# A mixture-of-experts stage that adds straight into the output, with a bound on the row index

## The chip, the core and the metric

The kernel runs on one core of a Trainium2 chip. The engines are named as the profile names them: PE (TensorE, matrix products and transposes), DVE (VectorE), ACT (ScalarE), POOL (GpSimd) and SP (SyncE, which here only starts transfers). Each engine works through its own list of instructions in order and waits at semaphores for the others. Transfers go through sixteen DMA engines; those with a list of row indices are started by POOL, whose software writes their descriptors, and nearly all others by SP. The metric is the time of one execution on the device, in microseconds (us).

## The reference

The input is x with 4 batches of 512 tokens and 256 features, all in 32-bit floats. Three residual steps follow each other:

```
x = x + 0.5 * ffn(layernorm(x))
x = x + attention(layernorm(x))          # 16 heads, low-rank queries and keys, rotary part
x = x + 0.5 * ffn(layernorm(x))

def ffn(x):                              # 8 experts, each token goes to 2 of them
    w, idx = top_k(x @ gate, 2);  w = softmax(w)
    h = silu(x @ w0[e]) * (x @ w1[e])    # 256 -> 512, for each chosen expert e
    return sum over the chosen e of  w[e] * (h @ wo[e])     # 512 -> 256
```

Both ffn steps use the same weights. Every token takes part in two experts, so each ffn step adds 4096 weighted rows into 2048 rows.

## The kernel before, in words

**Tiles.** For each of the two ffn stages (f = 0 before the attention, f = 1 after it) the (token, expert) pairs are sorted by expert into tiles of 128 slots. There are always 36 tiles. Four of them are shared: their lower 64 slots belong to one expert and their upper 64 to another. The rest have one expert each. `list_tiles` makes, for each tile, a column of row indices (`idx`; for shared tiles two columns in `half_idx`, one for each half) and a column of weights. A slot that holds no token gets an index from 2048 up, a "spare" row behind the tokens; the slots of the other half in `half_idx` point to spare rows too. Therefore the normed tokens `xn_d` and the sums `acc_d` in DRAM have more than 2048 rows (`NTOK` is 2048, `P` is 128), and `clear` writes zeros to the spare rows at the start, on POOL's queue.

**One tile.** `ffn_tiles` runs over the tiles. For each one, `gather` (POOL, indirect DMA, L1057) fetches 128 rows of `xn_d`; `turn` transposes them on PE; `hidden` makes the two hidden products and `it`; `turn_hidden` transposes `it`; `project` multiplies with wo, scales by the weights on DVE (`yo`, L1176) and hands the tile to `scatter` (POOL, indirect DMA with addition, L1153). For a shared tile there are two scatters, one with each column of `half_idx`; the second is put off to the next round (`later`). A tile's gather is issued two rounds ahead, and further ahead from tile `final` on. PE's order is fixed by hand: the hidden product of tile j, the transposes of tile j+1, then the projection of tile j-1.

**Order of the scatters.** Two scatters may add to the same rows, so each waits until the one before it has landed. The scatters form a chain on POOL, in which every step lasts from the start of one to the start of the next.

**Stage one** adds to `acc_d[0]`, into which x was copied. **The attention** loads x per batch from there, adds its own result in SBUF, and `finish_x` (SP) writes each batch to `acc_d[1]`.

**Stage two** has 17 tiles that are full and need the first three batches only, then 8 tiles in turn shared and full (tiles 17 to 24), then 11 more (tiles 25 to 35, `final` is 25). The first 25 tiles add to `acc_d[1]`. When tile 24 has been projected, SP copies `acc_d[1]` into the output in four pieces (L1192); the output is the kernel's result in DRAM, `flat_out` in the code. Tiles 25 to 35 then add to the output itself. They come after the copy in the chain; `HELD = 2` puts the scatters of tiles 25 and 26 off until that of tile 27, so that the gathers of the next tiles get ahead of them in POOL's list. For tiles from 25 on `list_tiles` makes indices that stay below 2048, also in tiles that no expert uses (their weights are zero).

The lines that decide where a scatter goes:

```
direct = final is not None and j >= final
dst = flat_out if direct else acc_d[f][: res["rows"] + two_rows, :]
...
if not direct or j >= final + HELD:
    scatter(held)
```

Of the kernel before, what the change touches and what calls it, by code (L numbers as in the profile page):

```python
# [9 lines left out]
F32 = mybir.dt.float32  # L10
# [6 lines left out]
P = 128  # L17
# [25 lines left out]
def kernel(  # L43
# [18 lines left out]
    nc = tc.nc  # L62
    B, S, D = x.shape
# [8 lines left out]
    NTOK = B * S  # L72
# [27 lines left out]
    qp = ctx.enter_context(tc.tile_pool(name="q", bufs=4))  # L100
    pp = ctx.enter_context(tc.tile_pool(name="p", bufs=2 * NT + 1))
    ptp = ctx.enter_context(tc.tile_pool(name="pt", bufs=2 * NT))
    ap = ctx.enter_context(tc.tile_pool(name="o", bufs=2))
    dp = ctx.enter_context(tc.tile_pool(name="dram", bufs=1, space=bass.MemoryType.DRAM))
# [3 lines left out]


    xn_d = [dp.tile([NTOK + P, D], F32, name=f"xn_d{f}") for f in range(2)]  # L110
    acc_d = [dp.tile([NTOK + 2 * P, D], F32, name=f"acc_d{f}") for f in range(2)]


    tab_d = [dp.tile([P * P, 2], F32, name=f"tab_d{f}") for f in range(2)]
# [2 lines left out]
    def rows(t, b):  # L117
        return t[b * S : (b + 1) * S, :].rearrange("(t p) d -> p t d", p=P)

    xs = {}  # L120

    def load_x(b, src):
        xs[b] = xpool.tile([P, NT, D], F32, tag="x", name="x")
        nc.sync.dma_start(xs[b], src)
# [53 lines left out]
    half_idx = counted("half_idx", [P, 2, NSHARED], [[P, 2], [0, NSHARED]], NTOK, 1, I32)  # L178
# [35 lines left out]
    nc.gpsimd.memset(zero, 0.0)  # L214

    def clear():
        for t in (xn_d[0], acc_d[0], xn_d[1], acc_d[1]):
            for r in range(NTOK, t.shape[0], P):
                nc.gpsimd.dma_start(t[r : r + P, :], zero)
        for t in tab_d:  # L220
            nc.gpsimd.dma_start(t.rearrange("(c s) v -> c (s v)", s=P), zero)
# [281 lines left out]
    class Phase:  # L503
# [17 lines left out]
        def scatter(self, s, k, t):  # L521

            nc.gpsimd.memset(self.between, 0.0)
            put = nc.gpsimd.indirect_dma_start(
                out=tab_d[self.f],
                out_offset=bass.IndirectOffsetOnAxis(ap=s["s_i"][:, k, t : t + 1], axis=0),
                in_=s["pair"][:, k, t, :],
                in_offset=None,
            )

            for other in self.written:
                tc.declare_no_dep(put.ins, other.ins, reason="other slots")
            self.written.append(put)
# [502 lines left out]

        return res, parts()

    HELD = 2
    flat_out = out.rearrange("b s d -> (b s) d")  # L1040

    def ffn_tiles(f, jobs, final=None):

# [96 lines left out]
        def turn_hidden(it):  # L1143
# [4 lines left out]
            nc.scalar.copy(iT, pt)  # L1148
            return iT

        def scatter(these):
            for dst, idx, y in these:
                nc.gpsimd.indirect_dma_start(  # L1153
                    out=dst,
                    out_offset=bass.IndirectOffsetOnAxis(ap=idx, axis=0),
                    in_=y,
                    in_offset=None,
                    compute_op=ALU.add,
                )
            these.clear()  # L1160

        def project(j, off, iT):
            res, i = jobs[j]
            py = ps_p.tile([P, D], F32, tag="p", name="py")
            two = shared(j)
            for m in range(MC):
                first_half(two, py, iT[:, m, :], w_sb[2][:, bass.ds(off + m * D, D)], m, MC)
                if two:
                    wo = copies[j][2 * DC + m // 2][:, m % 2 * D : (m % 2 + 1) * D]
                    second_half(py, iT[:, m, :], wo, m, MC)  # L1170
            copies.pop(j, None)
            direct = final is not None and j >= final

            pool, tag = (qp, "q") if direct else (ptp, "pt")
            y = pool.tile([P, D], F32, tag=tag, name="yo")
            nc.vector.tensor_scalar_mul(y, py, res["w"][:, i : i + 1])  # L1176
            two_rows = P if two else 0
            dst = flat_out if direct else acc_d[f][: res["rows"] + two_rows, :]
            idx = res["idx"][:, i : i + 1]
            if two:  # L1180

                held.append((dst, half_idx[:, 0, i : i + 1], y))
                later.append((dst, half_idx[:, 1, i : i + 1], y))
            else:
                held.append((dst, idx, y))
            if not direct or j >= final + HELD:
                scatter(held)
            if final is not None and j == final - 1:

                for r in range(0, NTOK, NTOK // 4):  # L1190
                    r = slice(r, r + NTOK // 4)
                    nc.sync.dma_start(  # L1192
                        flat_out[r, :].rearrange("(p r) d -> p (r d)", p=P),
                        acc_d[f][r, :].rearrange("(p r) d -> p (r d)", p=P),
                    )

        held, later = [], []
        gather(0)
        gather(1)
        yield -1  # L1200
# [3 lines left out]
        for j in range(n):  # L1204
            gather(j + 2)
            if final is not None and j >= final:

                gather(j + 3)
                if j > final:
                    gather(j + 4)  # L1210
            scatter(later)
            if j == n - 1:

                off, it = hidden(j, lambda: project(*todo))
                todo = None
            else:
                off, it = hidden(j)
            yield j
            turn(j + 1)
            yield j  # L1220
            if todo is not None:
                project(*todo)
            yield j
            todo = (j, off, turn_hidden(it))
            yield j
# [240 lines left out]
    def finish_x(i):  # L1466
        b, h = items[i]
        if h == NH - 1:
            nc.sync.dma_start(rows(acc_d[1], b), xs[b])

    def rest_of(res, n):

# [24 lines left out]
    for half in range(2):  # L1497
# [2 lines left out]

    nc.sync.dma_start(mark_d, list_a["w"][:, :n_a])
    nc.sync.dma_start(
        acc_d[0][:NTOK, :].rearrange("(p r) d -> p (r d)", p=P),
        x.rearrange("b s d -> (b s) d").rearrange("(p r) d -> p (r d)", p=P),
    )
    load_attention()
# [9 lines left out]
    for j in tiles:  # L1516
        place = place + 1 if place < 4 else 1
        beside.at(place)
        if j < n_a - 2:
            beside.step(3)  # L1520
            if j == n_a - 3 and place == 4:
                beside.finish()
        elif j == done + 1 and place == 1:
            load_x(0, rows(acc_d[0], 0))
        elif j == done + 2 and place == 1:
            beside.add(prepare(0), put_queries(0), put_queries(1))
        elif j > done + 2:
            beside.step(2 if place % 2 == 0 else 1)
        if j == len(jobs) - 1:
            if place == 1:  # L1530
                beside.finish()
            put_scores(place - 1)
            put_divide(place - 1)
    load_x(1, rows(acc_d[0], 1))
    for k in range(NT, NT + LEAD):
        put_scores(k)
        put_divide(k)
# [19 lines left out]
    for i, (b, h) in enumerate(items):  # L1557
        if h == 2:
            if b > 0:
                load = None  # L1560
                if b + 1 < B:
                    load = lambda b=b: load_x(b + 1, rows(acc_d[0], b + 1))
                routed = {}
                beside.add(route_one(two, b - 1, routed, load))
            if b + 1 < B:
                beside.add(prepare(b + 1))
            if b > 0:
                beside.add(scatter_one(two, routed))
            if b == B - 1:
                beside.add(listing)  # L1570
        for kc in range(NT):

            at = NT * (h % 2) + kc
            beside.at(at, at in (6, 7, 0, 1), LITTLE if late and ROOM[at] < 1.0 else ROOM[at])
            k = (i + 1) * NT + LEAD + kc
            if at != 1 or i == 0:
                put_scores(k)
            if at == 0 and i > 0:

                put_scores(k + 1)  # L1580
                put_weigh(i - 1, range(NT))
                put_divide(k)
                beside.step(PARTS[at])
            if at == 5:

                put_divide(k - 1)
            pts[i, kc] = turn_probs(probs[i], kc)
            for f in late:
                f()
            late.clear()  # L1590
            if at == 1:
                asked.add(put_queries(i // 2 + 2))
                beside.step(PARTS[at])
            elif at == 4 and h % 4 == 1 and i > 1:
                late.append(put_out(i - 2, 0))
            elif at == 6 and h % 4 == 1 and i > 1:
                late.append(put_out(i - 2, 1))
                late.append(lambda i=i: finish_x(i - 2))
            asked.step(ASKED[at])
            if at == 0 and i == 0:  # L1600
                put_divide(k)
            if at > 1 or at == 0 and i == 0:
                beside.step(PARTS[at])
        probs.pop(i)
# [87 lines left out]
```

## Time and profile before

| | |
|---|---|
| time, three runs | 1111.03 us median (1108.27 to 1111.64) |
| the profiled execution | 1107.51 us, with a span of 1105.7 us |
| mean clock granted to PE | 0.99 |
| busy: PE, DVE, ACT, POOL | 1053.1, 562.1, 476.5, 586.7 us |
| POOL: indirect gathers of 128 rows (L1057) | 72, mean 1006 ns |
| POOL: indirect scatters with addition (L1153) | 53 + 16 to `acc_d`, 11 to the output; 1582, 1575 and 1569 ns |
| scatter, issue to landing (median) | 3.7 to 3.8 us |
| copy of sums to the output (SP) | 4 transfers of 512 KB, 5.6 us to landing |

A row of POOL's DMA_INDIRECT tells how long POOL took for the instruction; the data lands later. The time to landing is counted from the issue. In a timeline, a number in square brackets is how long the engine sat idle before the instruction, followed by what ended that idle time; "issue" means that nothing shown in the profile ended it.

### The profile page before, as it was taken

The numbers are of one execution on the slowest core, as the hardware profiler recorded it, in microseconds if no ns is written. First come the engines' busy times: TensorE is split into PE (matmuls) and PEld (weight loads), VectorE is DVE, ScalarE is ACT, GpSimd is POOL, SyncE is SP. The second block draws the span as 40 slices with busy tenths as digits, with TensorE's granted clock in tenths as the row PEclk, the third lists the DMA queues.
The fourth block names the chain that finished last, engine by engine and source line by source line (L and its number), as shares of the span: only waits on it lengthen the run. The fifth ranks groups of instructions, "written<-read, shape, count | busy, mean of one in ns | idle before, by whom it ended". The sixth has DMA issues, their size and how long they took to land. (4 is left out here: it accounts for less than half of the span.)

```text
span 1105.7 us, 14702 instructions
## 1 busy us (share of the span) xinstructions
PE 1053.1 (95%) x4738; PEld 598.2 (54%) x4738; DVE 562.1 (51%) x1329; ACT 476.5 (43%) x1030; POOL 586.7 (53%) x655
## 2 busy tenths in 40 slices
PE   4899999999999999999999999999999899999994
PEld 3566555666545555455455545554555566655662
DVE  6563222334566565676666766666855342322221
ACT  3622432222555556545565554556545231144120
POOL 4345455466556555536774546864574247444442
PEclk8999999999999999999999999999999999999998
DMA  9973233322100000100000100001000224223422
GB/s 315 366 189 48 45 49 52 67 34 39 34 1 1 1 1 1 58 1 1 1 2 20 39 1 1 1 1 39 2 6 1 86 50 45 45 48 53 129 44 24
DMA packets 44043, 53.57 MB, mean 48 GB/s; under 512 B 10720, under 2 KB 36704, under 8 KB 43872
## 3 DMA queue, kind: packets, MB, share of 16 engines
q0 software_dynamic: 16960, 22.07, 12.6%
q1 hardware_dynamic: 26736, 30.55, 8.6%
q8 instruction: 40, 0.66, 0.2%
q14 instruction: 35, 0.29, 0.1%
q10 hardware_dynamic: 272, 0.01, 0.0%
HBM read 34.74 MB, written 22.07 MB: 51 GB/s over the span
## 5 line engine op out<-in xcount | busy, mean ns | idle before, releaser
L1104 PE MATMUL h<-w_sb,xT 128*128 (+1 forms) x576 | 260.3, 594 | 2.5 <-DVE xT L1072 1.9
L1355 PE MATMUL ps<-k,q 128*128 128x512 f32 x512 | 259.8, 600 | 0.8 <-ACT pr L1365 0.8
L1363 DVE TENSOR_REDUCE nm<-ps 128x1 f32<-128x512 f32 x256 | 175.0, 687 | 74.6 <-PE ps L1355 70.1
L1365 ACT ACTIVATE pr<-ps,nm 128x512 f32<-128x512 f32 x210 | 144.2, 687 | 129.0 <-DVE nm L1363 101.7
L1372 POOL TENSOR_SCALAR pr<-pr,sm 128x512 f32<-128x512 f32 x210 | 142.4, 694 | 69.8 <-DVE sm L1370 68.5
L1140 DVE TENSOR_TENSOR it<-g,h 128x512 f32<-128x512 f32 x72 | 49.5, 688 | 221.2 <-PE h L1104 174.6
L1104 PEld LDWEIGHTS h<-w_sb,xT 128*128 128x128 f32 (+1 forms) x576 | 100.4, 184 | 109.6 <-issue 103.4
L1378 PEld LDWEIGHTS pt<-ident,pr 128*128 128x128 f32 x840 | 102.9, 141 | 103.7 <-issue 64.8
L1153 POOL DMA_INDIRECT acc_d<-yo,idx x53 | 83.9, 1582 | 140.3 <-DVE yo L1176 73.7
L1148 ACT COPY iT<-pt_i 128x512 f32<-128x512 f32 x72 | 42.3, 587 | 246.0 <-PE pt_i L1146 246.0
L1378 PE MATMUL pt<-ident,pr 128*128 128x128 f32 x840 | 135.5, 275 | 4.2 <-ACT pT L1385 3.8
L1104 PE MATMUL py<-w_sb,iT 128*128 (+1 forms) x576 | 136.9, 381 | 1.4 <-ACT iT L1148 1.4
L1391 PE MATMUL po<-pT,low 128*64 128x512 f32 x512 | 116.9, 598 | 4.7 <-ACT pr L1365 4.6
L1383 DVE COPY pT<-pt 128x512 f32<-128x512 f32 x128 | 87.4, 683 | 55.0 <-PE pt L1378 55.0
L1241 POOL TENSOR_TENSOR tsin<-tsin,sin_sb 128x512 f32<-128x512 f32 x36 | 46.5, 1293 | 126.1 <-DVE tsin L1239 123.9
L1104 PEld LDWEIGHTS py<-w_sb,iT 128*128 128x128 f32 (+1 forms) x576 | 100.5, 184 | 18.2 <-ACT iT L1148 2.4
L1355 PEld LDWEIGHTS ps<-k,q 128*128 128x128 f32 x512 | 82.4, 190 | 44.1 <-issue 19.4
L1057 POOL DMA_INDIRECT xg<-xn_d,idx x72 | 72.4, 1006 | 30.1 <-issue 15.6
L1385 ACT COPY pT<-pt 128x512 f32<-128x512 f32 x128 | 74.1, 579 | 15.3 <-PE pt L1378 15.3
L1391 PEld LDWEIGHTS po<-pT,low 128*64 128x64 f32 x512 | 33.9, 136 | 83.5 <-issue 56.5
L1137 ACT ACTIVATE g<-h 128x512 f32<-128x512 f32 x72 | 43.0, 597 | 59.2 <-PE h L1104 56.2
L1176 DVE TENSOR_SCALAR yo<-py,wt 128x256 f32<-128x256 f32 x72 | 34.8, 483 | 63.6 <-PE py L1104 55.4
(234 smaller groups left out, 1329.2 us busy)
## 6 DMA issues: line engine op xcount, KB each, us to landing
w_sb<-in_L_ffn_w_kernel_dram SPq DMA_DIRECT2D x8, 1024.0 KB, 13.7
w_sb<-in_L_ffn_wo_kernel_dram SPq DMA_DIRECT2D x5, 1024.0 KB, 14.5
xn_d<-xn SPq DMA_DIRECT2D x12, 256.0 KB, 4.3
x<-_attn_hidden_states_dram SPq DMA_DIRECT2D x4, 512.0 KB, 10.1
x<-acc_d SPq DMA_DIRECT2D x4, 512.0 KB, 3.9
acc_d<-x SPq DMA_DIRECT2D x4, 512.0 KB, 3.0
out_dram<-acc_d SPq DMA_DIRECT2D x4, 512.0 KB, 5.6
xg<-xn_d,idx POOLq DMA_INDIRECT x72, 2.8
```

What stands on the lines that cost most here:

```text
L1057: nc.gpsimd.indirect_dma_start(out=xg[j], out_offset=None, in_=xn_d[f][: res["rows"], :], in_offset=bass.IndirectOffsetOnAxis(ap=res["idx" ...
L1104: nc.tensor.matmul(to[r], lhsT=lhsT[:, r], rhs=rhs, start=(k == 0), stop=(k == last - 1))
L1140: nc.vector.tensor_mul(it, g, ph[1])
L1153: nc.gpsimd.indirect_dma_start(out=dst, out_offset=bass.IndirectOffsetOnAxis(ap=idx, axis=0), in_=y, in_offset=None, compute_op=ALU.add,)
L1355: nc.tensor.matmul(ps, lhsT=qT[:, t * P : (t + 1) * P], rhs=st[b]["k"][h % 2], start=True, stop=True,)
L1363: nc.vector.tensor_reduce(nm, ps, AX.X, ALU.max, negate=True)
L1365: nc.scalar.activation(pr, ps, AF.Exp, bias=nm, accum_out=sm[:, t : t + 1])
L1372: nc.gpsimd.tensor_scalar(pr, pr, sm[:, t : t + 1], 1.0, ALU.mult, ALU.mult)
L1378: nc.tensor.transpose(pt[:, t * P : (t + 1) * P], probs[t][:, kc * P : (kc + 1) * P], ident)
L1383: nc.vector.tensor_copy(s, pt)
L1385: nc.scalar.copy(s, pt)
L1391: nc.tensor.matmul(po[j * RANK : (j + 1) * RANK], lhsT=st[b]["low"][:, kc, 1, :], rhs=pts[j], start=(kc == 0), stop=(kc == NT - 1),)
```

## The change

Stage two adds to the output from its first tile on. `finish_x` writes x after the attention into the output's rows instead of `acc_d[1]`. The copy from `acc_d[1]` to the output, the tensor `acc_d[1]`, the two transfers that cleared its spare rows, and `HELD` with its list are gone. The output has no spare rows, so all scatters of stage two are given a bound on the index: a row whose index is above 2047 is left out and is no error. In the built program this is one more register operand on each of the 40 scatters of stage two, with one instruction on POOL that sets the register. Stage one keeps its sums and its spare rows, and has no bound.

```
-    acc_d = [dp.tile([NTOK + 2 * P, D], F32, name=f"acc_d{f}") for f in range(2)]
+    acc_d = dp.tile([NTOK + 2 * P, D], F32, name="acc_d")
...
-        for t in (xn_d[0], acc_d[0], xn_d[1], acc_d[1]):
+        for t in (xn_d[0], acc_d, xn_d[1]):
             for r in range(NTOK, t.shape[0], P):
                 nc.gpsimd.dma_start(t[r : r + P, :], zero)
...
+        skip = {"bounds_check": NTOK - 1, "oob_is_err": False} if f else {}
+
         def scatter(these):
             for dst, idx, y in these:
                 nc.gpsimd.indirect_dma_start(
...
                     compute_op=ALU.add,
+                    **skip,
                 )
...
-            direct = final is not None and j >= final
-            pool, tag = (qp, "q") if direct else (ptp, "pt")
+            pool, tag = (qp, "q") if final is not None and j >= final else (ptp, "pt")
...
-            dst = flat_out if direct else acc_d[f][: res["rows"] + two_rows, :]
-            idx = res["idx"][:, i : i + 1]
+            dst = flat_out if f else acc_d[: res["rows"] + two_rows, :]
             if two:
-                held.append((dst, half_idx[:, 0, i : i + 1], y))
+                scatter([(dst, half_idx[:, 0, i : i + 1], y)])
                 later.append((dst, half_idx[:, 1, i : i + 1], y))
             else:
-                held.append((dst, idx, y))
-            if not direct or j >= final + HELD:
-                scatter(held)
-            if final is not None and j == final - 1:
-                for r in range(0, NTOK, NTOK // 4):
-                    r = slice(r, r + NTOK // 4)
-                    nc.sync.dma_start(
-                        flat_out[r, :].rearrange("(p r) d -> p (r d)", p=P),
-                        acc_d[f][r, :].rearrange("(p r) d -> p (r d)", p=P),
-                    )
+                scatter([(dst, res["idx"][:, i : i + 1], y)])
...
-            nc.sync.dma_start(rows(acc_d[1], b), xs[b])
+            nc.sync.dma_start(rows(flat_out, b), xs[b])
```

More of the change, by code (lines that the diff above doesn't have):

```diff
@@ L1037, in list_tiles @@
         return res, parts()
-    HELD = 2
     flat_out = out.rearrange("b s d -> (b s) d")
@@ L1177, in project @@
             two_rows = P if two else 0
-            dst = flat_out if direct else acc_d[f][: res["rows"] + two_rows, :]
-            idx = res["idx"][:, i : i + 1]
+            dst = flat_out if f else acc_d[: res["rows"] + two_rows, :]
             if two:
-                held.append((dst, half_idx[:, 0, i : i + 1], y))
+                scatter([(dst, half_idx[:, 0, i : i + 1], y)])
                 later.append((dst, half_idx[:, 1, i : i + 1], y))
             else:
-                held.append((dst, idx, y))
-            if not direct or j >= final + HELD:
-                scatter(held)
-            if final is not None and j == final - 1:
-                for r in range(0, NTOK, NTOK // 4):
-                    r = slice(r, r + NTOK // 4)
-                    nc.sync.dma_start(
-                        flat_out[r, :].rearrange("(p r) d -> p (r d)", p=P),
-                        acc_d[f][r, :].rearrange("(p r) d -> p (r d)", p=P),
-                    )
-        held, later = [], []
+                scatter([(dst, res["idx"][:, i : i + 1], y)])
+        later = []
         gather(0)
@@ L1502 @@
     nc.sync.dma_start(
-        acc_d[0][:NTOK, :].rearrange("(p r) d -> p (r d)", p=P),
+        acc_d[:NTOK, :].rearrange("(p r) d -> p (r d)", p=P),
         x.rearrange("b s d -> (b s) d").rearrange("(p r) d -> p (r d)", p=P),
@@ L1523 @@
         elif j == done + 1 and place == 1:
-            load_x(0, rows(acc_d[0], 0))
+            load_x(0, rows(acc_d, 0))
         elif j == done + 2 and place == 1:
@@ L1533 @@
             put_divide(place - 1)
-    load_x(1, rows(acc_d[0], 1))
+    load_x(1, rows(acc_d, 1))
     for k in range(NT, NT + LEAD):
@@ L1561 @@
                 if b + 1 < B:
-                    load = lambda b=b: load_x(b + 1, rows(acc_d[0], b + 1))
+                    load = lambda b=b: load_x(b + 1, rows(acc_d, b + 1))
                 routed = {}
```

## The prediction

> **What bounds the kernel now.** I read the page's busy times and slices first, then the chain that ended last, then POOL's timeline over the end of stage two, then the times of `yo` on DVE, because `yo` is what each scatter waits for.
>
> ```profile
> span 1105.7 us, 14702 instructions
> ...
> PE 1053.1 (95%) x4738; PEld 598.2 (54%) x4738; DVE 562.1 (51%) x1329; ACT 476.5 (43%) x1030; POOL 586.7 (53%) x655
> ...
> L1153 POOL DMA_INDIRECT acc_d<-yo,idx x53 | 83.9, 1582 | 140.3 <-DVE yo L1176 73.7
> ...
> L1057 POOL DMA_INDIRECT xg<-xn_d,idx x72 | 72.4, 1006 | 30.1 <-issue 15.6
> ```
>
> PE is busy for 95% of the span; nothing that the change touches is on PE. The two POOL rows give the price of a list of 128 rows: 1.01 us for a gather, 1.58 us for a scatter with addition.
>
> ```profile
> 1092.43 1.55 DMA out_dram<-yo,idx
> 1093.99 2.81 issue
> 1096.80 1.77 POOLq L1688
> ```
>
> In the chain that ended last, the end hangs on the last two scatters, not on PE.
>
> ```profile
> 1036.63 1.59 POOL L1153 DMA_INDIRECT acc_d<-yo,idx  x1 [2.85 <-DVE xT L1072]
> ...
> 1051.30 1.61 POOL L1153 DMA_INDIRECT out_dram<-yo,idx  x1 [7.96 <-issue]
> 1056.00 1.58 POOL L1153 DMA_INDIRECT out_dram<-yo,idx  x1 [3.09 <-issue]
> ...
> 1087.95 1.55 POOL L1153 DMA_INDIRECT out_dram<-yo,idx  x1 [2.97 <-DVE yo L1176]
> 1092.43 1.55 POOL L1153 DMA_INDIRECT out_dram<-yo,idx  x1 [2.93 <-DMA out_dram<-yo,idx]
> 1097.02 1.55 POOL L1153 DMA_INDIRECT out_dram<-yo,idx  x1 [3.03 <-issue]
> ```
>
> ```profile
> 1040.53 2.45 SPq L1192 DMA_DIRECT2D out_dram<-acc_d  x4
> ```
>
> This is the chain of scatters from tile 24 (1036.63) to tile 35 (1097.02). Between the two lies the copy, issued at 1040.53; the scatter of tile 25 starts only at 1051.30. From there ten steps take 45.72 us, 4.57 us each.
>
> ```profile
> 1036.64 0.48 DVE L1176 TENSOR_SCALAR yo<-py,wt 128x256 f32<-128x256 f32 x1 [0.86 <-PE py L1104]
> ...
> 1083.20 0.48 DVE L1176 TENSOR_SCALAR yo<-py,wt 128x256 f32<-128x256 f32 x1 [0.87 <-PE py L1104]
> 1087.08 0.48 DVE L1176 TENSOR_SCALAR yo<-py,wt 128x256 f32<-128x256 f32 x1 [3.40 <-PE py L1104]
> 1092.96 0.48 DVE L1176 TENSOR_SCALAR yo<-py,wt 128x256 f32<-128x256 f32 x1 [3.42 <-PE py L1104]
> ```
>
> These are `yo` of tiles 25, 33, 34 and 35. From 25 to 33 they come every 5.82 us ((1083.20 - 1036.64) / 8), which is PE's pace. Tile 25 was ready at 1037.12 and scattered 14.2 us later. The chain gains 5.82 - 4.57 = 1.25 us on PE per tile but has not caught up: the last `yo` ends at 1093.44, its scatter starts at 1097.02.
>
> **The change part by part.**
>
> *Copy and held scatters removed.* Where a scatter waits for DVE alone it starts 0.28 us after `yo` (`yo` ends at 988.62, scatter at 988.90; 982.64 and 982.92). Without the copy, the chain goes on from tile 24 at 4.57 us a step: tile 25 at 1041.20, 26 at 1045.77, 27 at 1050.34, 28 at 1054.91. `yo` of tile 28 ends at 1054.58 and allows 1054.86, so the chain has caught up there. After that each scatter waits for its own `yo`: tile 33 at 1083.96, 34 at 1088.53 (one step later; its `yo` allows 1087.84), 35 at the later of 1093.10 and 1093.44 + 0.28 = 1093.72. What follows the last scatter to the end of the span (8.68 us) stays. Gain: 1097.02 - 1093.72 = 3.30 us. What is late next is the last `yo`, which is PE's time. The four issues leave SP, where nothing is queued behind them.
>
> *Scatters of tiles 25 and 26 no longer held.* On POOL they now stand ahead of gathers for tile 31 and later. These gathers start behind them by about 1047; the burst before ended at 1043.33. PE turns those rows after 1065. Cost nothing; the cover is about 18 us.
>
> *First scatter of stage two now waits for batch 3's rows too.* SP issues that store at 871.20, and such stores land in 3.0 us. The first scatter starts at 884.19. Cost nothing, with 10 us to spare.
>
> *Two clears of 128 KB removed at the start.* They take 1.07 us on POOL, and their going lets the next clears and the store of batch 1's rows (17.60) go earlier. The reader is the first gather at 40.23, which waits for DVE's `off`; gain nothing by this way. The DMA engines then move 353 GB/s, so 256 KB less is 0.74 us of traffic; PE waits for a gather there once, 0.8 us at 46.20. Bounds 0 and -0.7; I take 0, because routing on DVE sets that stretch.
>
> *The register for the bound.* 40 instructions on POOL, each ahead of a wait that lasts 0.3 to 4.9 us: hidden by it.
>
> *The bound itself, e per scatter.* No row of before has one. From below: nothing, or a gain, since the eight scatters of shared tiles have at least 64 of 128 rows to leave out; if POOL's time went by rows, half of 1.58 us. That gain would lie between tiles 17 and 24, where the chain has room to catch up, and reach the end with nothing. From above: 1.01 us, a whole second run through 128 indices, by the gather's row. The addition, a feature that does cost, adds 1.58 - 1.01 = 0.57 us. Payload adds nothing: the scatter into the routing table, 8 bytes a row, takes 1.00 us (the fuller list of groups has it) against 1.01 us for the gather's 1 KB.
>
> ```profile
> L524 POOL DMA_INDIRECT tab_d<-cut x40 | 39.8, 996 | 10.9 <-issue 6.6 <-DVE cut L678 4.0 <-DMA acc_d<-yo,idx 0.2
> ```
>  A comparison of an index adds no transfer, so I hold it nearest to this last pair and take e = 0, keeping 0 and 1.01 as the ends.
>
> What e does: it lengthens every step of the chain. The chain alone, from tile 17 on, would start tile 35 at 1036.63 + 11 x 4.57 + 22e = 1086.9 + 22e (11 steps up to tile 24, 11 after it), and over the last two steps at 1093.10 + 2e. Up to e = 0.31 the last `yo` (1093.72) still decides, and the only loss is e once, on the last scatter itself. Beyond that the end moves by 22e + e.
>
> Here a rule can be weighed. The rows say that a feature on a list of 128 indices may cost POOL 0.00 or 0.57 us. The Trainium skill, GPSIMD Engine Reference, section 7, gives compare-and-select bodies on that engine 2.03 cycles an element; at the 1.2 GHz that the Trainium skill states for GpSimd (Trainium Kernel Development and Optimization, NeuronCore Architecture), 128 comparisons are an estimated 0.22 us. By this the sum would be -3.1 us instead of -3.3. The Trainium skill, DMA: Bandwidth & Descriptors, section on the anatomy of one DMA, calls descriptor generation small and puts most of the time on the receipt of the write; the trace agrees only in part, with 1.58 us of the 3.8 us to landing spent on POOL.
>
> **Sum.** 0 + 0 - 3.30 + 0 = -3.3 us against the profiled execution: 1107.5 - 3.3 = 1104.2. The median of the three runs shown, 1111.03, lies 3.5 us above that execution; I carry the difference over: 1111.0 - 3.3 = 1107.7 us.
>
> **The rivals.**
>
> *A: as forecast, e up to 0.31.* -3.3 to -3.0 us, up to 0.7 us better by the start: 1107.0 to 1108.0. For it: the copy's hole in the chain is plain, and eight tiles lie between the point of catching up and the end.
>
> *B: the bound takes back most of it, e from 0.31 to 0.58.* The end is set by 1086.9 + 23e; at e = 0.44 the gain is used up, at 0.57 (the price of the addition) the end is 1100.0, +3.0 us. Time 1108 to 1114. For it: the one feature whose price shows costs 0.57.
>
> *C: slower, the chain becomes the bound of stage two.* From e = 0.58 the loss passes 3.3 us. At e = 1.01 the last scatter ends 13.1 us later: 1086.9 + 23.2 - 1097.0. Time 1114 to 1124. For it: between tiles 17 and 24 three scatters take 12.9 us (988.90 to 1001.83), while PE makes their two tiles in 12.24 us (`yo` at 988.14 and 1000.38); the chain has no room there now. Against it: leaving out rows makes just these scatters shorter, if anything.
>
> *D: no change: the end waits for something else.* If a transfer other than the last scatter set the end, the 3.3 us would be lost: 1111.0. The trace shows none after 1097.02.
>
> **How the numbers follow.** A 0.60, B 0.14, C 0.24, D 0.02. A change of 0.3%, 3.3 us, is about what a measurement of this kernel can tell from none. A sits on that bound: with the start's up to 0.7 us above and e below, I give it 0.41 faster and 0.19 within. B and D are within, but for 0.01 at each end of B. Faster 0.42, same 0.33, slower 0.25. A's own range is 1106 to 1109. The range of all reaches down to 1104.5, the forecast from a somewhat quicker execution (the lowest run was 2.8 us under the median), and up to 1116, a little into C; about 0.18 is left out above and 0.02 below.
>
> **What would show it.** Right: no copy on SP; the scatter of tile 25 near 1041, that of tile 28 starting 0.3 us after its `yo`, the last one 0.3 us after the last `yo` (now 3.58 us); stage two's scatters at 1.55 to 1.65 us; PE's `yo` times as before. Wrong: scatters of 1.9 us or more, a step of the chain above 5 us, a last scatter that again waits for a landing, gathers that keep PE waiting, or scatters with left-out rows that take longer than full ones.

## The result and the profile after

The changed kernel takes 1106.81 us (median of 22 runs, 1104.77 to 1114.36), the kernel before 1110.79 us (22 runs, 1108.27 to 1113.67). The ratio is 0.9971 with a 95% interval of 0.9961 to 0.9982. By this ratio the gain is 3.2 us, between 2.0 and 4.3 us; the two medians lie 4.0 us apart. Forecast were 3.3 us, which the prediction called about the least that can be told from no change; the interval lies clear of 1.

The page of the changed kernel, its span, busy time, and the two groups of scatters of 128 rows:

```profile
span 1105.5 us, 14732 instructions
PE 1055.3 (95%) x4738; PEld 598.9 (54%) x4738; DVE 561.2 (51%) x1329; ACT 476.5 (43%) x1030; POOL 584.1 (53%) x653
...
L1155 POOL DMA_INDIRECT out_dram<-yo,idx x32 | 50.7, 1585 | 89.1 <-DVE yo L1178 60.1
L1155 POOL DMA_INDIRECT acc_d<-yo,idx x32 | 50.4, 1576 | 82.8 <-DVE yo L1178 37.0
```

The scatters of stage two now have the bound and take POOL 1585 ns. Those of stage one do not have it and take 1576 ns. The clean comparison is within stage two, between the kernel before and the same kernel with the bound (an experiment below): 1591, 1569 and 1581 ns without the bound for full tiles into `acc_d`, full tiles into the output and shared tiles, and 1591, 1569 and 1581 ns with it. The bound costs POOL nothing that can be seen.

The span, 1105.5 us, is only 0.2 us below that of before. The two executions differ ahead of stage two, where the kernels do the same work but for the two clears at the start: the first `yo` of stage two starts at 883.43 us before and at 886.08 us after. Here are these two lines of DVE's timelines, before and then after:

```profile
883.43 0.48 DVE L1176 TENSOR_SCALAR yo<-py,wt 128x256 f32<-128x256 f32 x1 [0.21 <-PE py L1104]
```

```profile
886.08 0.48 DVE L1178 TENSOR_SCALAR yo<-py,wt 128x256 f32<-128x256 f32 x1 [0.21 <-PE py L1103]
```

Single spans therefore do not show a change of 3 us here. What shows it is a stretch inside the stage: from the first `yo` of stage two to its last scatter it is 213.59 us before (1097.02 - 883.43) and 210.82 us after (1096.90 - 886.08). That is 2.77 us less and not 3.30, because the last `yo` comes 0.53 us later behind the first one than before (210.06 us instead of 209.53); in that stretch PE waits once for a gather, 0.34 us at 938.92, which it did not do before.

POOL's timeline of the changed kernel, scatters of tiles 24, 25, 27, 28, 33, 34 and 35:

```profile
1038.64 1.59 POOL L1155 DMA_INDIRECT out_dram<-yo,idx  x1 [2.67 <-DVE it L1139]
...
1043.23 1.60 POOL L1155 DMA_INDIRECT out_dram<-yo,idx  x1 [0.39 <-issue]
...
1052.45 1.58 POOL L1155 DMA_INDIRECT out_dram<-yo,idx  x1 [1.73 <-DVE yo L1178]
...
1058.04 1.58 POOL L1155 DMA_INDIRECT out_dram<-yo,idx  x1 [2.72 <-DVE yo L1178]
...
1087.14 1.55 POOL L1155 DMA_INDIRECT out_dram<-yo,idx  x1 [4.27 <-DVE yo L1178]
1091.72 1.55 POOL L1155 DMA_INDIRECT out_dram<-yo,idx  x1 [3.02 <-DMA out_dram<-yo,idx]
1096.90 1.55 POOL L1155 DMA_INDIRECT out_dram<-yo,idx  x1 [3.63 <-DVE yo L1178]
```

And `yo` of tiles 25, 28 and 33 to 35 in DVE's timeline:

```profile
1039.82 0.48 DVE L1178 TENSOR_SCALAR yo<-py,wt 128x256 f32<-128x256 f32 x1 [0.86 <-PE py L1103]
...
1057.28 0.48 DVE L1178 TENSOR_SCALAR yo<-py,wt 128x256 f32<-128x256 f32 x1 [0.87 <-PE py L1103]
...
1086.38 0.48 DVE L1178 TENSOR_SCALAR yo<-py,wt 128x256 f32<-128x256 f32 x1 [0.87 <-PE py L1103]
1090.26 0.48 DVE L1178 TENSOR_SCALAR yo<-py,wt 128x256 f32<-128x256 f32 x1 [3.40 <-PE py L1103]
1096.14 0.48 DVE L1178 TENSOR_SCALAR yo<-py,wt 128x256 f32<-128x256 f32 x1 [3.42 <-PE py L1103]
```

The hole between tiles 24 and 25 is gone: one step of 4.59 us instead of 14.67. At tile 28 the scatter starts 0.28 us after its `yo` (1057.76 to 1058.04), so the chain has caught up with PE. The last one starts 0.28 us after the last `yo` has ended (1096.62 to 1096.90); before, it was 3.58 us.

### The profile page after: what moved, and what is told of

The parts are those of the page before. It is cut to its first block, busy times and chain, and to the rows that moved or that the text cites. A ratio compares the mean times of both kernels' runs of the same rounds, so it can differ in the third digit from the quotient of the medians.

```text
span 1105.5 us, 14732 instructions
## 1 busy us (share of the span) xinstructions
PE 1055.3 (95%) x4738; PEld 598.9 (54%) x4738; DVE 561.2 (51%) x1329; ACT 476.5 (43%) x1030; POOL 584.1 (53%) x653
## 3 DMA queue, kind: packets, MB, share of 16 engines
q0 software_dynamic: 16864, 21.03, 12.1%
## 5 line engine op out<-in xcount | busy, mean ns | idle before, releaser
L1155 POOL DMA_INDIRECT out_dram<-yo,idx x32 | 50.7, 1585 | 89.1 <-DVE yo L1178 60.1
L1155 POOL DMA_INDIRECT acc_d<-yo,idx x32 | 50.4, 1576 | 82.8 <-DVE yo L1178 37.0
```

Of the source, the lines that this page charges most:

```text
L1155: nc.gpsimd.indirect_dma_start(out=dst, out_offset=bass.IndirectOffsetOnAxis(ap=idx, axis=0), in_=y, in_offset=None, compute_op=ALU.add, * ...
```

## The experiments

The table gives, for each kernel, the ratio to the kernel before on the same chip with its 95% interval, and two numbers from its profiled execution: how late the last scatter starts after the last `yo` has ended, and the time from the first `yo` of stage two to the last scatter.

| kernel | ratio | last scatter late by | stage two |
|---|---|---|---|
| before | 1 | 3.58 us | 213.59 us |
| changed | 0.9971 (0.9961 to 0.9982) | 0.28 | 210.82 |
| changed, again | 0.9978 (0.9960 to 0.9995) | 0.28 | 210.85 |
| changed, a third time | 0.9979 (0.9965 to 0.9994) | 0.28 | 211.63 |
| before, copy twice | 1.0091 (1.0063 to 1.0119) | 6.18 | 221.94 |
| before, no holding | 0.9997 (0.9978 to 1.0015) | 4.41 | 214.41 |
| changed, with holding | 0.9967 (0.9943 to 0.9991) | 0.29 | 210.59 |
| before, with the bound | 0.9957 (0.9932 to 0.9981) | 2.01 | 212.01 |
| the same, again | 0.9979 (0.9962 to 0.9997) | 2.00 | 212.82 |
| changed, one empty scatter more | 1.0007 (0.9989 to 1.0025) | 0.28 | 210.94 |
| changed, four more | 1.0034 (1.0011 to 1.0057) | 6.43 | 217.18 |
| changed, clears put back | 0.9961 (0.9941 to 0.9981) | 0.28 | 210.85 |
| changed, bound in stage one too | 0.9928 (0.9900 to 0.9956) | 0.28 | 210.95 |
| changed, gathers of stage one earlier | 0.9950 (0.9926 to 0.9974) | 0.29 | 211.82 |

### The copy, taken twice

```
-                for r in range(0, NTOK, NTOK // 4):
+                for r in 2 * list(range(0, NTOK, NTOK // 4)):
```

> The kernel before with the copy of the sums made twice (the second time over the same rows, so it waits for the first). Theory, the copy sets the end only through the hole it leaves in the chain of scatters: the scatter of tile 25 moves from 14 us behind its yo to 20 to 24 us behind it, and the whole delay, 6 to 10 us, appears again at the last scatter (3.6 us behind the last yo becomes some 6 to 13) and in the time: 1117 to 1121 us. Rival, the copy costs by its traffic or not at all, and the gain came from elsewhere (the start, the bound): time within 2 us of before.

SP's timeline of this kernel, then POOL's (tiles 24 and 25), then PE's waits over the end of the stage:

```profile
1049.23 10.88 SPq L1192 DMA_DIRECT2D out_dram<-acc_d  x8
```

```profile
1045.31 1.59 POOL L1153 DMA_INDIRECT acc_d<-yo,idx  x1 [2.83 <-DVE yo L1176]
...
1066.55 1.61 POOL L1153 DMA_INDIRECT out_dram<-yo,idx  x1 [14.54 <-issue]
```

```profile
PE pt_x L1069 <- DMA xg<-xn_d,idx: 3.7, 2, 3.3
```

Tile 25 is scattered 21.3 us behind its `yo` (which ends at 1045.22) instead of 14.2 us, and the time grows by 0.91%, 10 us. The median of 1123.31 us lies 2 us above the range expected, on a chip where the kernel before took 1111.96. The delay does not all come back where I had put it: the last scatter is only 2.60 us later behind its `yo`, and the last `yo` itself comes 5.75 us later behind the first one of the stage (215.28 us instead of 209.53). Together these are the 8.35 us by which stage two is longer. Of the 5.75 us, 3.7 us are PE's waits for gathers that stand on POOL behind the waiting scatters. The products behind the longer of these waits are slow as well: eight products of `py` take 3.44 us there instead of 1.89, and the clock granted to PE is 0.83 from 1080 to 1090 us, after 1.00 from 1060 to 1080. So the larger hole costs time, as the theory has it, but the greater part of it comes by the later `yo` and not by the way that the theory named: at 21 us behind its `yo` the gathers issued ahead no longer cover it.

### The holding alone, both ways

In the kernel before:

```
-    HELD = 2
+    HELD = 0
```

> The kernel before with HELD = 0: the scatters of tiles 25 and 26 are issued with their own tiles, the copy stays. Theory: the chain still starts again only when the copy has landed, so tile 25 is scattered some 14 us behind its yo, the last scatter stays 3 to 3.6 us late, PE loses under 1 us on gathers behind the waiting scatters, time within 0.2% of before. Rival, the holding makes the delay: the time falls by 2 us or more, as with the whole change.

In the changed kernel:

```
-                scatter([(dst, res["idx"][:, i : i + 1], y)])
+                held.append((dst, res["idx"][:, i : i + 1], y))
+                if final is None or j < final or j >= final + 2:
+                    scatter(held)
...
-        later = []
+        later, held = [], []
```

> The changed kernel with the holding put back (tiles 25 and 26 scattered with tile 27), no copy. Theory: tile 25 is scattered by about 1045 (in the times of the profile before), the chain catches up with PE by tile 31, last scatter 0.3 us behind the last yo, time that of the changed kernel within 0.15%. Rival, half of the gain or more came from dropping the holding: last scatter 1.5 us or more late, time nearer to before.

Without holding, the kernel before keeps its time (0.9997) and its late end (4.41 us, where 3 to 3.6 were expected). With holding, the changed kernel keeps its gain (0.9967) and its punctual end. The gain does not come from the holding. A held scatter is only later in POOL's list, behind two more gathers: in the changed kernel with holding, tile 25 is scattered 7.02 us after tile 24 instead of 4.59, still 6.9 us ahead of the `yo` of tile 27, and the chain makes the difference good by tile 29.

### The bound alone

The kernel before, with the index limit on the 40 scatters of stage two and nothing else changed:

```
+        skip = {"bounds_check": NTOK - 1, "oob_is_err": False} if f else {}
...
                     compute_op=ALU.add,
+                    **skip,
```

> The kernel before with the bound alone: all 40 scatters of stage two get the index limit 2047, destinations, copy, clears and the held scatters stay. It prices the bound by itself. If the bound is free on POOL (theory): scatters of stage two at 1.55 to 1.65 us, steps of the chain at 4.5 to 4.6 us after the copy, last scatter 3 to 3.6 us behind the last yo, time within 0.15% of before. If the bound had a price that the gain covered up (rival): scatters at 1.8 us or more and 5 us or more behind the last yo, time up by over 3 us. If left-out rows make POOL's work shorter (second rival): the eight scatters with half_idx near 0.8 us.

> The kernel before with the bound alone, a second time, because its first ratio, 0.9957, is larger than what its trace shows: there the step from the first to the second scatter of a shared tile fell from 4.0 to 3.4 to 3.9 us in three of four tiles, the copy could start earlier, and the last scatter was 2.0 us behind the last yo instead of 3.6, a gain of 1.6 us. Theory, that is all the bound does: ratio 0.998 to 0.9995, last scatter 1.7 to 2.3 us late. Rival, the bound is worth as much as the whole change: ratio 0.997 or less.

The page's lines on packets and on POOL's queue, kernel before:

```profile
DMA packets 44043, 53.57 MB, mean 48 GB/s; under 512 B 10720, under 2 KB 36704, under 8 KB 43872
q0 software_dynamic: 16960, 22.07, 12.6%
```

and kernel before with the bound:

```profile
DMA packets 44043, 52.79 MB, mean 48 GB/s; under 512 B 11488, under 2 KB 36704, under 8 KB 43872
q0 software_dynamic: 16960, 21.29, 12.1%
```

POOL's queue has as many packets as before, but 0.78 MB less, and 768 more packets are under 512 bytes. At 1 KB a row that is about 768 rows: a row that is left out still is a packet, a small one. POOL's time stays at 1581 ns for the scatters of shared tiles in stage two, half of whose rows or more are left out. Neither the price feared nor the halving happened.

The expectation of the first run, no change within 0.15% and an end that is 3 to 3.6 us late, failed. Some steps of the chain at the shared tiles got shorter. From the first to the second scatter of a shared tile the step had been 3.97, 4.00, 3.98 and 4.50 us; with the bound it is 3.97, 3.42, 3.73 and 4.49. Behind the second scatter of the third shared tile it fell from 4.55 to 3.46 us. Over tiles 17 to 24 the chain is 2.0 us shorter. The copy starts earlier, tile 25 is scattered 12.1 us behind its `yo` instead of 14.2 (13.0 in the second run), and the end is 2.0 us late instead of 3.58. The last scatter and the last `yo` of the first run, from POOL's and DVE's timelines:

```profile
1099.16 1.55 POOL L1155 DMA_INDIRECT out_dram<-yo,idx  x1 [3.04 <-issue]
```

```profile
1096.67 0.48 DVE L1179 TENSOR_SCALAR yo<-py,wt 128x256 f32<-128x256 f32 x1 [3.42 <-PE py L1104]
```

Over stage two the two runs gain 1.6 and 0.8 us. Their ratios, 0.9957 and 0.9979, ask for 4.8 and 2.3 us. The second ratio lies between the two expectations of its run, and its interval reaches into both. The rest isn't found in stage two, and this kernel's stage one is that of before; it stays open whether it is scatter among executions.

This matters for the whole change, which has the bound too. On the same two chips it gives 0.9967 (with holding) and 0.9979: by the whole time, the bound alone and the whole change can't be told apart. What tells them apart is the end of stage two in the traces, 2.0 us late with the bound and the copy, 0.28 us without the copy. No kernel here leaves the copy out without having the bound. That the chain would catch up at tile 28 or soon after without the bound too is the prediction's sum, and no run shows it by itself.

### Longer chain without a copy

One more scatter ahead of that of tile 25, with an index list that lies wholly above the bound, so that nothing is added to the output:

```
+    none = counted("none", [P, 1], [[0, 1]], NTOK, 1, I32)
...
+                if final is not None and final <= j < final + 1:
+                    scatter([(dst, none, y)])
                 scatter([(dst, res["idx"][:, i : i + 1], y)])
```

> The changed kernel with one more scatter ahead of that of tile 25, whose 128 indices all lie above the bound: nothing is added to the output, but the chain gets one more step. Theory: the extra step takes 2.5 to 4.6 us, the chain makes it good in two to four tiles at 1.25 us each, the last scatter stays 0.3 us behind the last yo, time that of the changed kernel (ratio to before 0.996 to 0.998). Rival, the chain has no slack: the time grows by the whole step. It also prices a scatter in which every row is left out: if POOL's time goes by the rows that are sent, well under 1 us; if every index costs the same, 1.5 to 1.65 us.

And with `final + 4`, ahead of each of tiles 25 to 28:

> The same with an extra empty scatter ahead of each of tiles 25, 26, 27 and 28: four more steps, no copy anywhere. With a step of s us the chain alone would start the last scatter at 1086.9 + 4 s, against 1093.72 by the last yo (times of the profile before). Theory, any delay of the chain before tile 35 beyond what ten tiles can make good comes back at the end: s of 3.5 gives a last scatter 7 us late and a time near 1114, s of 2.5 gives 3 us and 1110; the end then follows 1086.9 + 4 s with the measured s to within 1.5 us. Rival, it was the copy's 4 MB of traffic that cost: no bytes are moved here, so the time stays that of the changed kernel.

POOL's timeline of the kernel with four, over its first two pairs and at the last tile, whose `yo` is shown behind it:

```profile
1050.73 1.61 POOL L1156 DMA_INDIRECT out_dram<-yo,none  x1 [0.43 <-DVE it L1140]
1053.79 1.58 POOL L1156 DMA_INDIRECT out_dram<-yo,idx  x1 [1.44 <-DMA out_dram<-yo,none]
...
1058.42 1.58 POOL L1156 DMA_INDIRECT out_dram<-yo,none  x1 [1.72 <-DVE yo L1179]
...
1109.15 1.55 POOL L1156 DMA_INDIRECT out_dram<-yo,idx  x1 [2.99 <-issue]
```

```profile
1102.24 0.48 DVE L1179 TENSOR_SCALAR yo<-py,wt 128x256 f32<-128x256 f32 x1 [3.42 <-PE py L1104]
```

An empty scatter takes POOL 1.58 us, as a full one does, and its step is 3.06 us (1050.73 to 1053.79); the full one behind it takes 4.63 us. One extra step is made good by tile 30: the last scatter is punctual and stage two as long as without. Four are not: 4 x 3.0 us more in the chain make the chain alone end at 1086.9 + 12.1 = 1099.0 in the times of the profile before, 5.3 us behind the last `yo`'s 1093.72. Measured are 6.43 - 0.28 = 6.15 us, and 6.3 us in stage two (217.18 against 210.85), and the ratio is 0.56% above that of the changed kernel on the same chip (0.9978), 6.2 us. No bytes are copied here. Here the cost is the delay in the chain, without any traffic of a copy.

The time expected for one extra scatter was missed: 1.0007 instead of 0.996 to 0.998. Stage two did what was expected; its first `yo` came at 894.44 us, 7 us later than in the changed kernel on that chip (887.38). The two differ ahead of that by one small instruction on POOL and one small tile. An execution of the changed kernel as it is, on another chip, came as late (895.11), so this run doesn't show that the edit did it.

### The start, and stage one

The two clears put back, into a tensor that nothing reads:

```
+    spare_d = dp.tile([NTOK + 2 * P, D], F32, name="spare_d")
...
-        for t in (xn_d[0], acc_d, xn_d[1]):
+        for t in (xn_d[0], acc_d, xn_d[1], spare_d):
```

> The changed kernel once more, on the same chip as the two next ones: ratio to before 0.996 to 0.998, last scatter 0.3 us behind the last yo.

> The changed kernel with the two clears of 128 KB put back at the start (into a tensor that nothing reads). It prices the start alone. Theory: the store of batch 1's normed rows is a little later on POOL, routing on DVE sets the stretch, PE's first hidden product starts within 0.3 us of where it does without; time equal to the changed kernel within 0.15%. Rival, the 0.7 us by which the measured gain (4.0 us between medians) goes beyond the 3.3 us of the end comes from the start: time 0.5 to 0.8 us above the changed kernel, with the first gathers landing later.

With the clears it is not slower (1110.12 against 1112.94 us, intervals that overlap). PE's first hidden product starts at 47.18 us with them and at 47.24 to 48.27 us in the three executions without, so the forecast of 0.3 us was missed, though not because of a cost. The up to 0.7 us at the start do not show; a ratio with this interval can't rule them out.

Two versions that might be better, each from the changed kernel. The bound in stage one as well, without spare rows in the sums and without their clears:

```
-    acc_d = dp.tile([NTOK + 2 * P, D], F32, name="acc_d")
+    acc_d = dp.tile([NTOK, D], F32, name="acc_d")
...
-        for t in (xn_d[0], acc_d, xn_d[1]):
+        for t in xn_d:
...
-        skip = {"bounds_check": NTOK - 1, "oob_is_err": False} if f else {}
+        skip = {"bounds_check": NTOK - 1, "oob_is_err": False}
...
-            dst = flat_out if f else acc_d[: res["rows"] + two_rows, :]
+            dst = flat_out if f else acc_d[: min(res["rows"], NTOK), :]
```

> The changed kernel with the bound in stage one as well, without spare rows in the sums and without their two clears. Theory: stage one ends at PE's pace and its last scatter is followed by the attention's loads well ahead of need, so nothing is gained at the end; the start loses 1.1 us of POOL work that nothing waits for: equal to the changed kernel within 0.2%. Rival, POOL's chain in stage one holds PE up (its gathers wait behind scatters), and shorter steps there show: 1 to 3 us faster than the changed kernel.

And gathers of stage one a round earlier:

```
             gather(j + 2)
+            if f == 0 and j + 3 < n and "idx" in jobs[j + 3][0]:
+                gather(j + 3)
```

> The changed kernel with the gathers of stage one issued three rounds ahead instead of two, where their indices exist by then. The traces so far put the first yo of stage two anywhere from 883 to 894 us, and the differences arise between 60 and 300 us, where PE waits for gathers that stand on POOL behind a scatter that waits for a slow landing. Theory: those waits go, the first yo of stage two comes at 880 to 884 us and the time is 3 to 6 us below the changed kernel. Rival, the waits are set by the landing of the gathers themselves or by DVE's routing: no change beyond 0.2%.

The changed kernel on that chip:

> The changed kernel again, beside the other three on one chip: ratio to before 0.996 to 0.998, from the first yo of stage two to the last scatter 210.5 to 211.2 us (before 213.6).

Its ratio came as expected, 0.9979. Stage two took 211.63 us, 0.4 us over the range; PE waits 0.9 us for gathers in it.

Here the theory for the bound fell, and its rival came nearer, with a gain above its 1 to 3 us. POOL's timeline over a shared tile, the full one after it, and the next shared tile, in stage one of the changed kernel on that chip (no bound there):

```profile
132.12 1.58 POOL L1155 DMA_INDIRECT acc_d<-yo,half_idx  x1 [3.11 <-DVE yo L1178]
...
136.19 1.57 POOL L1155 DMA_INDIRECT acc_d<-yo,half_idx  x1 [1.18 <-DMA acc_d<-yo,half_idx]
140.71 1.57 POOL L1155 DMA_INDIRECT acc_d<-yo,idx  x1 [2.95 <-issue]
...
145.25 1.57 POOL L1155 DMA_INDIRECT acc_d<-yo,half_idx  x1 [1.65 <-issue]
```

and with the bound in stage one:

```profile
131.33 1.58 POOL L1155 DMA_INDIRECT acc_d<-yo,half_idx  x1 [3.10 <-DVE yo L1178]
...
134.73 1.57 POOL L1155 DMA_INDIRECT acc_d<-yo,half_idx  x1 [0.52 <-DMA acc_d<-yo,half_idx]
138.50 1.57 POOL L1155 DMA_INDIRECT acc_d<-yo,idx  x1 [2.20 <-issue]
...
143.57 1.57 POOL L1155 DMA_INDIRECT acc_d<-yo,half_idx  x1 [2.19 <-DVE yo L1178]
```

Three scatters take 13.13 us without the bound and 12.24 us with it, and 12.24 us is PE's time for the two tiles: the next shared tile waits for its `yo` again, not for a landing. Without the bound the chain falls behind, and the gathers in POOL's list with it. The stretch from 120 to 200 us (span of the stretch, then PE's busy time) of the changed kernel, of the one with the bound, and of the one with earlier gathers, one line of each:

```profile
120.00:200.00 80.00, 77.91 (x342) 42.99 (x338) 18.75 (x37) 25.42 (x46) 39.69 (x30) 0.98 0.33 49
```

```profile
120.00:200.00 80.00, 79.93 (x353) 44.25 (x350) 19.57 (x39) 25.81 (x47) 41.06 (x32) 1.00 0.24 40
```

```profile
120.00:200.00 80.00, 80.00 (x356) 45.60 (x355) 20.65 (x42) 24.97 (x45) 39.63 (x30) 1.00 0.33 51
```

PE idles 2.09 us in it in the changed kernel (1.0 and 1.4 us in its other two executions), 0.07 us with the bound and nothing with earlier gathers. The trace of the changed kernel used here is that of its longest run on this chip (1117.13 us), so the 2.09 us are the upper end. The bound in stage one gives 0.9928, on a chip where the changed kernel gave 0.9979: 1109.50 against 1113.54 us, the best kernel here, ahead of the changed kernel and of the kernel before by intervals that do not touch. Of these 4.0 us the stretch shown explains 1 to 2; the rest is not located. The edit also drops two clears and the spare rows; that clears show no cost was seen above, the spare rows were not tried apart. Earlier gathers give 0.9950, with an interval that overlaps that of the changed kernel, so a gain over it is not shown. The forecast first `yo` of stage two, 880 to 884 us, was missed (887.26): waits between 62 and 120 us remained, of which the longest, 2.9 us, is for DVE's routing table, which the rival had named. The two were not tried together.

## Why the prediction was right, point by point

*The hole left by the copy.* Right in place and size. Tile 25 was forecast 4.1 us behind its `yo` and came 2.9 us behind it, since the shared tiles ahead of it had become a little shorter; catching up at tile 28, the step that ties tile 34 to 33, and 0.28 us at the end came as worked out.

*The gain.* 3.30 us at the end were forecast. The last scatter moved by exactly that relative to the last `yo` (3.58 - 0.28), so the mechanism came as worked out. Lengthening the chain without a copy moves the end by 6.15 us where the chain's sum says 5.3: a delay in the chain is enough to make the end late. Doubling the copy makes stage two 8.35 us longer, but mostly by another way, PE's waits for gathers. That the whole time agrees as closely, 3.2 us by the ratio, is in part luck: the traces give 2.77 us over stage two, the interval reaches from 2.0 to 4.3 us, and the bound alone, with the copy in place, gives as good a ratio.

*Held scatters, first scatter's longer wait, register.* Nothing, as costed. The holding was tried from both sides. The first scatter of stage two starts 0.28 us after its `yo` (886.56 to 886.84), as before; the register was not tried apart from the bound.

*The bound on POOL.* e was taken as 0 between ends of 0 and 1.01 us; measured are 1569 to 1591 ns in stage two by the kind of tile and destination, the same with the bound and without it. The rivals that lived on e fall with that. The Trainium skill's GPSIMD Engine Reference, section 7, led to an estimate of 0.22 us for the comparisons; the measurement shows none of it. What the prediction had wrong is "reach the end with nothing" of the left-out rows: it fits the changed kernel, whose chain has slack after tile 24, but with the copy in place they were worth 0.8 us or more. Its two sentences on tiles 17 to 24, that the chain "has room to catch up" there and that it "has no room there now", do not go together either; the second one is right.

*The start.* Taken as 0, and the clears put back show no cost, within an interval wider than the 0.7 us in question.

*The other side.* "The chain has no room there now" (12.9 us against 12.24) was a correct reading of tiles 17 to 24. I drew from it only what could make the change slower. The same reading of stage one, whose four shared tiles go through the same chain (13.0 us for three scatters in the profile before, 124.62 to 137.63), would have pointed to the better kernel.

## What to carry to other kernels

Where transfers must follow each other, work out the chain as a line of its own: its step, the pace of what feeds it, and how far behind it is at each point. A delay in the middle costs only what the slack from there to the end does not make good. A change of 3 us can be seen in a single trace although the spans scatter more, if it is measured from an event inside the stage: here 213.6 us before and 214.4 without holding, against 210.6 to 211.8 for the changed kernel and those of its variants whose chain catches up. An edit can bring two causes at once, and the whole time alone did not tell the bound from the copy here; the place in the trace where each of them shows did. And a reading that a chain has no room says where to look for gains, not only for losses.

## What the runs showed of the hardware that I had not expected

- A row of a scatter with addition that is left out by the bound saves POOL nothing: 1.58 us whether none, half or all of the 128 rows are left out. It stays a packet, under 512 bytes. But a scatter with all rows left out lands sooner: the step behind a scatter is 4.6 us with all rows and 3.0 us with none. With half of the rows it is less even. In stage one the steps behind the scatters of a shared tile are 4.07 and 4.52 us without the bound and 3.40 and 3.77 us with it (the first shared tile of the two timelines above). In stage two of the changed kernel the steps behind the first scatters of the four shared tiles are 3.97, 3.39, 3.57 and 4.49 us, and those behind the second ones 4.51, 4.41, 4.59 and 4.27; before, the latter were 4.51, 4.42, 4.55 and 4.46. Why the two stages differ wasn't tried. The Trainium skill, DMA: Bandwidth & Descriptors, section on the anatomy of one DMA, fits a transfer with 2.0 us and its bytes at 436 GB/s; the 128 KB between a full and an empty scatter would be an estimated 0.3 us by this. Here they are about 1.6 us, for rows that are added and not only written.
- The time ahead of stage two scatters by 12 us between executions (first `yo` of stage two at 883 to 895 us), and by 9 us among the three of the changed kernel (886 to 895). Much of it arises between 60 and 200 us, where PE waits for gathers and for the routing table: 0.9 and 0.6 us in the profile before, 3.3 and 3.7 us in the latest execution of the changed kernel. The granted clock differs as well: from 62 to 120 us its mean is 1.00 in the profile before and 0.94 in that execution, and 0.83 in the 20 us behind its longest wait (100 to 120 us). In the kernel with the doubled copy it is 0.83 behind a wait of 3.3 us too. In both cases, then, a wait of over 3 us went with a lower granted clock behind it; whether it is the cause, and why the landings differ so much, wasn't tried.
